# Four layers in one core: rotary rows earlier, layer 0's second context through 128-byte runs, a folded router, and another split of the rotary product

## The chip, the cores and the metric

The kernel runs as one program on one core of a Trainium2 chip. The metric is the device time of one execution in microseconds, as the median of several runs. The core has five engines that run their own instruction streams in order: TensorE (PE, with its weight loads as PEld), VectorE (DVE), ScalarE (ACT), GpSimd (POOL) and SyncE (SP, which here only issues DMAs). An instruction that waits for a semaphore holds everything behind it on its own engine.

## The reference

Eight sequences of 128 tokens with 512 features go through four layers. Each is a cross attention to a context of 128 tokens and a feed-forward block, both added to x; each takes a plain layernorm of x. All is float32.

```python
x = x + L0_xattn(_layernorm(x), ctx, mask0, position_bias, ln_weight, ...)  # 32 heads of 128
x = x + L0_ffn(...)   # 512x512 plus low-rank experts, sparsemax gate
x = x + L1_xattn(...) # 8 small heads over 128-column patches
x = x + L1_ffn(...)   # int8
x = x + L2_xattn(_layernorm(x), ctx, ctx, pos, mask2, Wq, Wk, Wv, Wo)   # 32 q heads, 8 kv heads, rotary
x = x + L2_ffn(...)   # NF4 quantized weights, 1376 hidden
x = x + L3_xattn(...) # 32 q heads, 8 kv heads
x = x + L3_ffn(...)   # router of rank 16 over 64 experts, top 16
```

The parts that the change touches:

```python
# layer 0: the layernorm's result is normed again, and scaled per feature
x = x * rsqrt(mean(x**2) + EPS) * ln_weight        # then q = x @ w_q.T
k = ctx @ w_k.T; v = ctx @ w_v.T
# layer 2: rotary positions
cos, sin = cos_t[position_ids], sin_t[position_ids]
q = q * cos + rotate_half(q) * sin                 # rotate_half: concat(-x2, x1)
k = k * cos + rotate_half(k) * sin
# layer 3, feed-forward: router
q = einsum('bsd,rd->bsr', x, Wq_w)                 # 16 values a token
scores = einsum('bsr,er->bse', q, keys)            # 64 experts
```

## The kernel before

The eight sequences are worked in two halves of four (`HALF`), whose 512 token columns are one moving operand. Attention of layers 0 and 2 runs as a list of 128 units: layer 0's first half (eight groups of four heads), layer 0's second half, layer 2's first half, layer 2's second half. The unit loop is a software pipeline: while unit u is weighed (softmax times values), the scores of u+2 and the projections of u+3 are made. After a group's last head come its four output projections. A tile framework then orders the instructions of each engine and puts in the semaphores; what the source places early or late in the loop is a wish, which the built order follows in the main.

Work that is not attention of the running stage is put in a table by slot (`put(i, f)`); the unit loop calls `slot()` after each piece of projection and after each output projection, two a unit and eight more at a group's end, and each call takes the table's next entry. `drain()` empties the table at the end of a stage. In this way `l0_half(1)` prepares layer 0's second half, from unit 3 on, and `short_stages(hf)` runs layer 0's feed-forward, layer 1's attention and feed-forward and the next norm for half hf under the attention units of the next stage: half 0 under layer 0's second half, half 1 under layer 2's first half. The same calls also hand out steps of the NF4 quantization of layer 2's feed-forward weights, in which ScalarE (`ind`) and VectorE (`dq`) take turns. Those steps last into layer 2's second half. Then come layer 2's feed-forward and layer 3, whose loop runs over items (half, group, sequence) and has its feed-forward put between items by hand (`between`).

A matrix is turned in one of two ways. `transposed` (L191) uses four 128x128 products with the identity on TensorE and a copy out of PSUM. The other way is VectorE's 32x32 block transpose with a DMA that carries blocks: `blocks_sent` and `norm_sent` write blocks to DRAM and read them back in place; `runs_back` and `runs_turned` read 32-element runs of 128 bytes and turn them on VectorE afterwards. `xb_tile` is the layout that the block way leaves, and `chunk` lets a product read either layout.

What the steps of the prediction touch:

- `l0_ctx`, `l0_query`, `l0_turn`: the second half's context is loaded whole and turned on TensorE with a copy by ScalarE; x is loaded, normed twice, turned on TensorE and scaled by `lnw` on VectorE.
- `L1.__init__`: layer 1's weights, 14 small loads on SP, once for each half.
- `L2Inputs`: the mask of layer 2, the positions and the row numbers of all eight sequences; `gather` fetches a sequence's cos and sin rows by an indirect DMA of POOL, `turn` turns them on TensorE. All eight run at the end of `short_stages(0)`.
- `rope` (L711 to L717): VectorE takes the projection from PSUM times cos, then two half products with sin, each from the other half of the partitions; POOL adds. It is called 16 times for keys (L726) and 64 times for queries (L294). The scores (L322) wait for it.
- `F3.route` (L1117 on): four products of `wr` with x give 16 values a token, ScalarE copies them (`qr`), one product with `ke` gives 64 scores, and VectorE picks the top 16. Eight calls, four of them in the last 60 us.
- The SP queue issues nearly all loads of weights (`w`, a ring of 12 buffers; `wo`, 8) in one order with the block transfers.
- PSUM: two banks `mm` for projections in the main stream, three shared by the side work.

Of the kernel before, what the change touches and what calls it, by code (L numbers as in the profile page):

```python
# [62 lines left out]
def kernel(ctx: ExitStack, tc: tile.TileContext, a, out):  # L63
# [187 lines left out]
    def norm_sent(st, b, quarters=False):  # L251
        h = layernorm(st, b)
        view = "p (a b k) -> p a b k" if quarters else "p (b a k) -> p a b k"
# [112 lines left out]
    def l0_ctx(st, b):  # L366
        S.copy(ctxT[:, :, toks(b)], transposed(st, load_ctx(st, b)))
# [11 lines left out]
    def l0_query(st, b):  # L379
        load(x[b], a["x"][b])  # L380
        h = layernorm(st, b)
        r, _ = l0_rms(st, h)
        G.tensor_add(x[b], x[b], h)
        return r

# [131 lines left out]


# [6 lines left out]
    class L1:  # L525
        def __init__(self, st, hf):
# [4 lines left out]
            self.wqk = l1c.tile([P, 3, 64], F32, name="wqk")  # L531
            load(self.wqk, a["l1_wqkv"])
            self.wo = l1c.tile([P, P], F32, name="wo1")
            G.memset(self.wo, 0.0)
            for h in range(8):
                r = 32 * (h % 4) + 8 * (h // 4)
                load(self.wo[r:r + 8, :], a["l1_wo"][8 * h:8 * h + 8, :])
            self.bqk = l1c.tile([P, 1], F32, name="bqk")
            load(self.bqk[0:64, :], a["L1_xattn_bq"].unsqueeze(1))
            load(self.bqk[64:128, :], a["L1_xattn_bk"].unsqueeze(1))  # L540
            self.bv = l1c.tile([P, 64], F32, name="bv")
            load(self.bv, a["L1_xattn_bv"].unsqueeze(0).to_broadcast([P, 64]))
            self.bo = l1c.tile([P, 1], F32, name="bo")
            load(self.bo, a["L1_xattn_bo"].unsqueeze(1))
            hm = l1c.tile([P, 8], F32, name="hm")
            load(hm[64:128, :], a["headmask"])
            self.h4 = l1c.tile([P, 4], F32, name="h4")
            V.tensor_add(self.h4[64:128, :], hm[64:128, 0:4], hm[64:128, 4:8])
# [123 lines left out]
    class L2Inputs:  # L672
        def __init__(self, st):
            self.st = st
            self.pool = tc.tile_pool(name="l2c", bufs=1)
            l2c = self.l2c = self.pool.__enter__()
            mi = l2c.tile([P, B, P], I32, name="mi")
            load(mi, a["mask_ik0"])
            V.tensor_scalar(neg2, mi, 0.0, -BIG, ALU.is_equal, ALU.mult)
            pi = l2c.tile([P, B], I32, name="pi")  # L680
            for b in range(B):
                load(pi[:, b:b + 1], a["pos"][b // HALF, toks(b % HALF)].unsqueeze(1))

            pf = l2c.tile([P, B], F32, name="pf")
            wr = l2c.tile([P, B], F32, name="wr")
# [9 lines left out]
            self.row = l2c.tile([P, B], I32, name="row")  # L695
            V.tensor_copy(self.row, pf)
            self.cs = {}

        def gather(self, b):
# [3 lines left out]
                bass.IndirectOffsetOnAxis(ap=self.row[:, b:b + 1], axis=0))  # L703
# [7 lines left out]
    def rope(dst, mm, t):  # L711
# [3 lines left out]
        V.tensor_mul(r[0:64, :], mm[64:128, :], t[64:128, 1, :])  # L715
        V.tensor_mul(r[64:128, :], mm[0:64, :], t[0:64, 1, :])  # L716
        G.tensor_add(dst, dst, r)  # L717
# [376 lines left out]
    class F3:  # L1094
        def __init__(self, st, hf, f3, wr, ke, wa, wb):
            self.st, self.hf, self.f3, self.wr, self.ke, self.wa, self.wb = st, hf, f3, wr, ke, wa, wb
            self.xT = xt_tile()
            self.h, self.s, self.z, self.zt = {}, {}, {}, {}
# [17 lines left out]
        def route(self, b):  # L1116
            st, f3 = self.st, self.f3  # L1117
            mm = st.mm()
            for c in range(DC):
                T.matmul(mm[:16, :P], lhsT=self.wr[:, c, :], rhs=self.xT[:, c, cols(b)], start=c == 0, stop=c == DC - 1)  # L1120
            qr = f3.tile([16, P], F32, tag="qr", name="qr")
            S.copy(qr, mm[:16, :P])
            sc = st.sc()
            T.matmul(sc[:, 0, :64], lhsT=qr, rhs=self.ke, start=True, stop=True)
# [470 lines left out]
```

## Time and profile before

| what | value |
|---|---|
| median of 3 runs | 3034.03 us (3032.01 to 3035.2) |
| the profiled execution | 3032.72 us |
| its span, first to last instruction | 3030.9 us |
| mean granted TensorE clock | 1.000 |
| DMA read and written | 317.70 MB and 125.33 MB |
| layer 0, first half alone | up to about 550 us |
| layer 2's attention | about 1060 to 1840 us |
| layer 2's feed-forward | about 1840 to 2069 us |
| layer 3 | about 2069 us to the end |

In the profile's groups a line gives the source line, engine, operation and tiles, the count, then busy time and mean duration, then the idle time of the engine just ahead of these instructions and what ended it. A 128x512 float32 product counts as two MATMUL records, whose durations overlap; the distance of their starts is what they take of TensorE's time. In a timeline the columns are start and length in us, engine, line, operation, and in brackets the idle time ahead of it.

### The profile page before, as it was taken

How to read it: one execution, taken by the hardware profiler on the slowest of the kernel's cores; microseconds unless marked ns; L12 is line 12 of the kernel's file. 1: busy time of each engine (PE TensorE's matmuls, PEld its weight loads, DVE VectorE, ACT ScalarE, POOL GpSimd, SP SyncE). 2: the span in 40 equal slices, each digit the busy share in tenths (PEclk: the TensorE clock that was granted, in tenths of full speed). 3: DMA queues.
4: the chain of work that ended last, by engine and by line, in shares of the span. 5: the costliest groups of instructions: out<-in, count | busy, mean ns of one | idle time of the engine just before them, and what ended most of it. 6: DMA issues, size and time to landing. Idle time of an engine off the chain costs nothing.

```text
span 3030.9 us, 35307 instructions
## 1 busy us (share of the span) xinstructions
PE 2999.1 (99%) x10580; PEld 1641.3 (54%) x10584; DVE 1905.8 (63%) x3846; ACT 1336.5 (44%) x3775; POOL 444.7 (15%) x581
## 2 busy tenths in 40 slices
PE   9999999999999999999999999999999999999999
PEld 4544555544444465555555554446566666655554
DVE  5766677667786566887888882215545556555554
ACT  4555565435562433554555561003434343333332
POOL 2000000101110121332111110103111112111111
PEclk9999999999999999999999999999999999999999
DMA  7434444336555633655344433325565656665541
GB/s 219 135 116 123 125 131 122 106 116 169 166 164 164 193 105 98 181 177 169 123 150 122 131 121 105 93 84 157 174 190 174 189 167 196 202 182 175 169 146 47
DMA packets 459006, 445.45 MB, mean 147 GB/s; under 512 B 49568, under 2 KB 347296, under 8 KB 458304
## 3 DMA queue, kind: packets, MB, share of 16 engines
q1 hardware_dynamic: 420896, 357.18, 39.2%
q0 software_dynamic: 14880, 44.06, 5.0%
q10 hardware_dynamic: 23040, 41.95, 4.7%
q8 instruction: 86, 1.41, 0.2%
q14 instruction: 104, 0.85, 0.1%
HBM read 317.70 MB, written 125.33 MB: 146 GB/s over the span
## 4 chain that ended last, share of the span: by engine, by line
PE 86%; DVE 8%; ACT 2%; DMA 2%; issue 1%; POOL 0%; SPq 0%; ACTq 0%; DVEq 0%; POOLq 0%
PE mm L294 18%; PE mm L212 11%; PE tp L1000 7%; PE mm L429 7%; PE mm L1023 7%; PE po L212 7%; PE mm L958 5%; PE sc L1060 4%; PE pv L1083 4%; PE pv L342 3%; PE sc L322 3%; PE mm L967 2%; PE mm L726 1%; DVE dq L803 1%; ACT s L207 1%
## 5 line engine op out<-in xcount | busy, mean ns | idle before, releaser
L212 PE MATMUL mm<-w,o 128*128 128x512 f32 x1024 | 462.6, 595 | 2.1 <-ACT o L344 1.6
L792 ACT ACTIVATE ind<-nw,bounds 128x512 f32<-128x512 f32 (+2 forms) x495 | 345.2, 712 | 239.1 <-DVE dq L803 162.9
L294 PE MATMUL mm<-xT,w 128*128 128x512 f32 x768 | 346.8, 594 | 3.5 <-DVE rot L716 2.3
L803 DVE SCALAR_TENSOR_TENSOR dq<-ind,dq 128x512 f32<-128x512 f32 (+2 forms) x462 | 327.5, 709 | 27.1 <-ACT ind L792 9.1
L212 PEld LDWEIGHTS mm<-w,o 128*128 128x128 f32 x1024 | 188.7, 190 | 221.3 <-issue 206.9
L207 ACT ACTIVATE s<-s,nm 128x128 f32<-128x128 f32 x512 | 198.2, 388 | 100.3 <-DVE nm L313 96.2
L1023 PE MATMUL mm<-w,xT 128*128 128x512 f32 x512 | 234.7, 592 | 0.0
L294 PEld LDWEIGHTS mm<-xT,w 128*128 128x128 f32 x768 | 142.5, 190 | 170.2 <-issue 161.8
L294 PE MATMUL mm<-ctxT,w 128*128 128x512 f32 x512 | 230.3, 593 | 0.8 <-ACT ctxT L1338 0.8
L429 PE MATMUL mm<-w,ctxT 128*128 128x512 f32 x512 | 230.5, 593 | 0.0
L212 PE MATMUL po<-w,o 128*128 128x512 f32 x512 | 229.8, 592 | 0.0
L207 ACT ACTIVATE p<-sc,nm,rq 128x256 f32<-128x256 f32 x256 | 141.0, 560 | 162.2 <-DVE nm L1065 154.9
L160 POOL TENSOR_TENSOR rs<-rs,mhalf 128x1 f32<-128x1 f32 x64 | 38.1, 602 | 871.6 <-DVE rs L181 852.7
L212 PEld LDWEIGHTS po<-w,o 128*128 128x128 f32 x512 | 97.3, 190 | 121.2 <-issue 117.2
L322 PEld LDWEIGHTS sc<-k,q 128*128 128x128 f32 x1024 | 131.5, 191 | 53.9 <-issue 45.1
L1086 ACT COPY o<-pv 128x512 f32<-128x512 f32 x62 | 36.3, 585 | 278.5 <-PE pv L1083 259.2
L1064 DVE TENSOR_REDUCE nm<-sc 128x2 f32<-128x512 f32 x128 | 87.4, 688 | 109.3 <-PE sc L1060 106.8
L429 PEld LDWEIGHTS mm<-w,ctxT 128*128 128x128 f32 x512 | 95.3, 190 | 112.0 <-issue 110.5
L958 PE MATMUL mm<-xB,w 128*128 128x512 f32 (+1 forms) x352 | 152.1, 592 | 0.8 <-DVE x L213 0.8
L213 DVE TENSOR_TENSOR x<-x,mm 128x512 f32<-128x512 f32 x128 | 86.6, 677 | 104.4 <-PE mm L212 104.2
L294 PEld LDWEIGHTS mm<-ctxT,w 128*128 128x128 f32 x512 | 93.5, 190 | 100.4 <-issue 98.6
L344 ACT COPY o<-pv 128x512 f32<-128x512 f32 x128 | 74.2, 579 | 158.0 <-PE pv L342 157.9
(264 smaller groups left out, 4984.8 us busy)
## 6 DMA issues: line engine op xcount, KB each, us to landing
w<-in_l_wq SPq DMA_DIRECT2D x128, 256.0 KB
w<-in_l_wo SPq DMA_DIRECT2D x128, 256.0 KB
far<-tb SPq DMA_DIRECT2D x125, 256.0 KB
pt<-far SPq DMA_DIRECT2D x500, 64.0 KB
far<-tb SPq DMA_DIRECT2D x62, 512.0 KB
pt<-far SPq DMA_DIRECT2D x248, 128.0 KB
far<-tb SPq DMA_DIRECT2D x63, 384.0 KB
pt<-far SPq DMA_DIRECT2D x252, 96.0 KB
```

The lines of the kernel that those rows point to most:

```text
L207: S.activation(dst(h), src(h), AF.Exp, bias=negm[:, h:h + 1], scale=by, accum_out=su[:, h:h + 1])
L212: T.matmul(mm, lhsT=o(h), rhs=wo[h], start=h == 0, stop=h == 3)
L294: T.matmul(mm, lhsT=w[:, c, :], rhs=chunk(xT, c), start=c == 0, stop=c == DC - 1)
L322: T.matmul(sc[:, i, :], lhsT=self.q[:, i * P:(i + 1) * P], rhs=k[:, i * P:(i + 1) * P], start=True, stop=True)
L429: T.matmul(mm, lhsT=ctxT[:, c, toks(self.hf * HALF + i)], rhs=grp.wv[c], start=c == 0, stop=c == DC - 1)
L792: S.activation(ind, w, AF.Relu, bias=bounds[:n, i:i + 1], scale=(down + up)[i][1])
L803: V.scalar_tensor_tensor(dst, ind, step, dst, ALU.min, ALU.subtract if i == len(down) else ALU.add)
L958: T.matmul(mm[:n, :], lhsT=w[c][:, j * P:j * P + n], rhs=chunk(xT, c), start=c == 0, stop=c == DC - 1)
L1000: T.matmul(it.kv[:, s, :], lhsT=lhsT, rhs=it.wkv[c // 2][:, c % 2, :], start=c == 0, stop=c == DC - 1)
L1023: T.matmul(mq, lhsT=self.xT[it.hf][:, c, cols(it.b)], rhs=it.wq[c], start=c == 0, stop=c == DC - 1)
L1060: T.matmul(sc[:, i, :], lhsT=it.qT[2 * j + i], rhs=it.kT, start=True, stop=True)
L1083: T.matmul(pv, lhsT=it.v[:, j, :], rhs=it.pts[j], start=j == 0, stop=j == 1)
```

## The change

Seven edits, in the order of the diff below:

1. Layer 0's second half: the context comes straight from the input in 128-byte runs (`runs_back` on SP, four loads a sequence) and is turned by VectorE; the normed x goes out in blocks and comes back in blocks (`blocks_out`, a piece of `norm_sent` made a function; `norm_arrives`), and `l0_weigh` scales it by `lnw` on POOL. Its tile has the block layout. `l0_half(1)` begins at unit 10 in place of 3, with its steps spread over six slots a sequence in place of four.
2. Layer 1's weights are loaded once, from POOL's queue, at unit 6, into a pool that stays.
3. `L2Inputs` works one half at a time, in three steps: loads, row numbers and gathers, turns. Half 0's loads and gathers begin right after layer 1's attention, its turns at their old place; half 1's stand at the head of `short_stages(1)`.
4. `rope`: ScalarE copies the two halves of the projection, swapped, into `rot`; VectorE multiplies the whole tile by sin; POOL subtracts in place of adding.
5. `F3.route`: `router()`, called once ahead of item 31's other work, makes `wk`, the product of `wr` and `ke` (512 by 64); `route` then has four products with x as the stationary operand and 64 columns of `wk` moving.
6. The three products at the start that warm TensorE read a corner of the block tile.
7. `short_stages` has `turn_rows` and `gather_rows` in the table, and `load_l1` stands beside it.

```diff
@@ -251,4 +251,5 @@
     def norm_sent(st, b, quarters=False):
-        h = layernorm(st, b)
-        view = "p (a b k) -> p a b k" if quarters else "p (b a k) -> p a b k"
+        return blocks_out(st, layernorm(st, b), "p (a b k) -> p a b k" if quarters else "p (b a k) -> p a b k")
+    def blocks_out(st, h, view):
         tb = st.wide("sq" if st.name == "s" else "pt", (P, 4, DC, 32))
@@ -366,3 +367,6 @@
     def l0_ctx(st, b):
-        S.copy(ctxT[:, :, toks(b)], transposed(st, load_ctx(st, b)))
+        return runs_back(st, a["ctx_4096"][b], nc.sync)
+    def l0_ctx_turn(b, t):
+        runs_turned(ctxT[:, :, toks(b)], t)
@@ -385,2 +389,10 @@
+    def l0_send(st, b, r):
+        return blocks_out(st, r, "p (b a k) -> p a b k")
+    def l0_weigh(b):
+        i = 4 * (b % HALF)
+        t = xT0[1][:, i:i + 4]
+        G.tensor_mul(t, t, lnw.unsqueeze(1).unsqueeze(3).to_broadcast([P, 4, DC, 32]))
     def l0_turn(st, b, r):
...
@@ -530,20 +544,3 @@
             l1c = self.pools.enter_context(tc.tile_pool(name="l1c", bufs=1))
-            self.wqk = l1c.tile([P, 3, 64], F32, name="wqk")
-            load(self.wqk, a["l1_wqkv"])
...
-            self.h4 = l1c.tile([P, 4], F32, name="h4")
-            V.tensor_add(self.h4[64:128, :], hm[64:128, 0:4], hm[64:128, 4:8])
+            self.wqk, self.wo, self.bqk, self.bv, self.bo, self.h4 = l1_weights
             self.vt = l1c.tile([P, 4, 8, 32], F32, name="vt")
@@ -672,15 +669,21 @@
     class L2Inputs:
-        def __init__(self, st):
-            self.st = st
+        def __init__(self, st, hf):
+            self.st, self.hf = st, hf
             self.pool = tc.tile_pool(name="l2c", bufs=1)
             l2c = self.l2c = self.pool.__enter__()
-            mi = l2c.tile([P, B, P], I32, name="mi")
-            load(mi, a["mask_ik0"])
-            V.tensor_scalar(neg2, mi, 0.0, -BIG, ALU.is_equal, ALU.mult)
-            pi = l2c.tile([P, B], I32, name="pi")
-            for b in range(B):
-                load(pi[:, b:b + 1], a["pos"][b // HALF, toks(b % HALF)].unsqueeze(1))
+            if hf == 0:
+                self.mi = l2c.tile([P, B, P], I32, name="mi")
+                load(self.mi, a["mask_ik0"])
+            self.pi = l2c.tile([P, HALF], I32, name="pi")
+            for b in range(HALF):
+                load(self.pi[:, b:b + 1], a["pos"][hf, toks(b)].unsqueeze(1))
+            self.cs = {}
+        def rows(self):
+            l2c, pi = self.l2c, self.pi
+            if self.hf == 0:
+                V.tensor_scalar(neg2, self.mi, 0.0, -BIG, ALU.is_equal, ALU.mult)
-            pf = l2c.tile([P, B], F32, name="pf")
-            wr = l2c.tile([P, B], F32, name="wr")
+            pf = l2c.tile([P, HALF], F32, name="pf")
+            wr = l2c.tile([P, HALF], F32, name="wr")
             V.tensor_scalar(wr, pi, 0.0, float(MAXPOS), ALU.is_lt, ALU.mult)
...
@@ -714,5 +716,7 @@
         r = ap_.tile([P, 512], F32, tag="rot", name="rot")
-        V.tensor_mul(r[0:64, :], mm[64:128, :], t[64:128, 1, :])
-        V.tensor_mul(r[64:128, :], mm[0:64, :], t[0:64, 1, :])
-        G.tensor_add(dst, dst, r)
+        S.copy(r[0:64, :], mm[64:128, :])
+        S.copy(r[64:128, :], mm[0:64, :])
+        V.tensor_mul(r, r, t[:, 1, :])
+        G.tensor_tensor(dst, dst, r, ALU.subtract)
...
@@ -1119,9 +1123,5 @@
             for c in range(DC):
-                T.matmul(mm[:16, :P], lhsT=self.wr[:, c, :], rhs=self.xT[:, c, cols(b)], start=c == 0, stop=c == DC - 1)
-            qr = f3.tile([16, P], F32, tag="qr", name="qr")
-            S.copy(qr, mm[:16, :P])
-            sc = st.sc()
-            T.matmul(sc[:, 0, :64], lhsT=qr, rhs=self.ke, start=True, stop=True)
+                T.matmul(mm[:, :64], lhsT=self.xT[:, c, cols(b)], rhs=self.wk[:, c, :], start=c == 0, stop=c == DC - 1)
             s = f3.tile([P, 64], F32, tag="s3", name="s3", bufs=4)
-            V.tensor_copy(s, sc[:, 0, :64])
+            V.tensor_copy(s, mm[:, :64])
             t8 = st.small(8, "t8")
@@ -1253,6 +1253,15 @@
             now[0] = 0
+            def ctx_load(b):
+                box[b, 0] = l0_ctx(side, b)
+            def send(b):
+                box[b, 1] = l0_send(side, b, box[b])
             for i, b in enumerate(batches(hf)):
-                put(4 * i, l0_ctx, side, b)
-                put(4 * i + 1, query, b)
-                put(4 * i + 3, lambda b: l0_turn(side, b, box[b]), b)
+                put(6 * i, ctx_load, b)
+                put(6 * i + 2, query, b)
+                put(6 * i + 4, lambda b: l0_ctx_turn(b, box[b, 0]), b)
+                put(6 * i + 4, send, b)
+                put(6 * i + 7, lambda b: norm_arrives(xT0[1], b, box[b, 1]), b)
+                put(6 * i + 9, l0_weigh, b)
@@ -1268,2 +1277,17 @@
+            def gather_rows(i, hf):
+                put(i, begin, "l2", L2Inputs, hf)
+                call(i + 2, "l2", "rows")
+                for b in batches(hf):
+                    call(i + 3 + b % HALF // 2, "l2", "gather", b)
+            def turn_rows(i):
+                for b in batches(hf):
+                    call(i + b % HALF, "l2", "turn", b)
+                put(i + HALF + 1, lambda: o["l2"].pool.__exit__(None, None, None))
+            if hf:
+                gather_rows(0, hf)
+                turn_rows(10)
             put(0, begin, "f0", F0, hf)
@@ -1292,2 +1316,4 @@
             put(t, lambda: o["l1"].pools.close())
+            if hf == 0:
+                gather_rows(t + 1, hf)
             put(t + 1, begin, "f1", F1, hf)
@@ -1311,7 +1337,25 @@
             if hf == 0:
-                put(t + 1, begin, "l2", L2Inputs)
-                for b in range(B):
-                    call(t + 1 + b, "l2", "gather", b)
-                    call(t + 5 + b, "l2", "turn", b)
-                put(t + 13, lambda: o["l2"].pool.__exit__(None, None, None))
+                turn_rows(t + 1)
+        def load_l1():
+            l1w = sub_pool("l1w", 1)
+            wqk = l1w.tile([P, 3, 64], F32, name="wqk")
+            G.dma_start(wqk, a["l1_wqkv"])
...
+            h4 = l1w.tile([P, 4], F32, name="h4")
+            V.tensor_add(h4[64:128, :], hm[64:128, 0:4], hm[64:128, 4:8])
+            l1_weights.extend((wqk, wo, bqk, bv, bo, h4))
@@ -1328,8 +1372,9 @@
             unit.far = False
-        xT0 += [xt_tile(), xt_tile()]
+        xT0 += [xt_tile(), xb_tile()]
-        V.memset(xT0[1][:, 0, :], 0.0)
+        dummy = xT0[1][:, 0:4].rearrange("p a c j -> p (a c j)")
+        V.memset(dummy, 0.0)
         idle = side.mm()
         for i in range(3):
-            T.matmul(idle, lhsT=xT0[1][:, 0, 0:P], rhs=xT0[1][:, 0, :], start=True, stop=True)
+            T.matmul(idle, lhsT=dummy[:, 0:P], rhs=dummy, start=True, stop=True)
         of = {b: (main, side)[b // 2] for b in batches(0)}
@@ -1364,4 +1409,7 @@
             turning[0] = 8 * NG - 4 <= u < 8 * NG
-            if u == 3:
+            if u == 10:
                 l0_half(1)
+            if u == 6:
+                with tc.issue_after(mark[0].ins):
+                    load_l1()
             if not unit.far:
@@ -1435,2 +1483,16 @@
     load(ke, a["f3_keys"])
+    wk = l3c.tile([P, DC, 64], F32, name="wk3")
+    def router():
+        tp = late.tp()
+        for c in range(DC):
+            T.transpose(tp[:16, c, :], wr[:, c, :], ident)
+        wrt = f3.tile([P, D], F32, tag="z3", name="z3")[:16, :]
+        S.copy(wrt, tp[:16].rearrange("r c p -> r (c p)"))
+        mm = late.mm()
+        for c in range(DC):
+            T.matmul(mm[:, 64 * c:64 * c + 64], lhsT=wrt[:, c * P:(c + 1) * P], rhs=ke, start=True, stop=True)
+        S.copy(wk, mm[:, :4 * 64].rearrange("p (c e) -> p c e", c=DC))
     wa = l3c.tile([P, DC, 512], F32, name="wa")
```

## The prediction

> **What bounds the kernel now.** I read the page's busy row first, then the busy time by stretch, then the waits of TensorE in the one stage that has any, then durations by shape and two timelines.
>
> ```profile
> PE 2999.1 (99%) x10580; PEld 1641.3 (54%) x10584; DVE 1905.8 (63%) x3846; ACT 1336.5 (44%) x3775; POOL 444.7 (15%) x581
> ```
>
> TensorE is without work for 31.8 us of 3030.9. So time goes only if TensorE instructions go, or if one of those 31.8 us goes. Where they lie, by stretch (columns: stretch, length, then busy time of PE, PEld, DVE, ACT, POOL with counts, granted clock, DMA share, GB/s):
>
> ```profile
> 50.00:550.00 500.00, 500.00 (x1578) 255.47 (x1577) 357.34 (x658) 294.53 (x660) 11.30 (x11) 1.00 0.41 121
> ...
> 1220.00:1320.00 100.00, 97.14 (x510) 54.00 (x509) 84.73 (x146) 59.42 (x232) 33.62 (x46) 1.00 0.62 179
> 1320.00:1420.00 100.00, 96.71 (x520) 55.26 (x519) 82.52 (x147) 55.37 (x220) 33.13 (x47) 1.00 0.60 174
> ...
> 1660.00:1760.00 100.00, 99.77 (x398) 57.95 (x397) 84.83 (x134) 59.17 (x168) 16.44 (x12) 1.00 0.44 129
> ...
> 2640.00:2955.00 315.00, 315.00 (x996) 185.68 (x995) 166.74 (x406) 114.74 (x314) 52.57 (x66) 1.00 0.56 171
> ```
>
> In layer 0 (50 to 550) and layer 3 TensorE never stops: there only removed TensorE work counts. In layer 2 (1060 to 1840) the stretches leave 19.6 us idle, with VectorE at 80 to 85% and ScalarE at 55 to 60%. What TensorE waits for there:
>
> ```profile
> PE tp L191 <- DVE h L184: 2.7, 3, 1.3
> PE pv L342 <- DMA pt<-far: 2.5, 3, 1.0
> PE mm L294 <- DVE rot L716: 2.3, 4, 1.2
> PE sc L322 <- POOL q L717: 2.2, 2, 1.2
> PE pv L611 <- DVE s L593: 1.7, 2, 1.1
> ```
>
> No wait is long; most are VectorE coming late, and 4.5 us is the rotary chain itself (rot, then q). The granted clock is 1.00 throughout.
>
> **Layer 0's second context.** Sixteen transposes of the context and sixteen of the normed x leave TensorE.
>
> ```profile
> L191 PE MATMUL tp<-ident,h 128*128 128x128 f32 x84 | 12.6, 275 | 3.2 <-DVE h L184 3.2
> ```
>
> The 275 ns overlap. In the timeline the work behind a group of four starts 0.43 us after the group does (122.08, then 122.51), so 8 groups give 8 x 0.434 = **-3.5 us**, all on the path, since this stretch has no idle. Nothing of it is lost to layout: a 128x512 product that reads the block layout (xB, 596 ns) costs what one with the plain layout does (594). In return VectorE gets eight block transposes (0.70 each) and loses four scalings (0.685): +2.9 us in a stretch where it is 71% busy. ScalarE loses 4 x 0.58. POOL gets 4 products with lnw (1.27 us, like its other 128x512 tensor operations) and, for layer 1's weights, 14 issues of about 0.6 us: some 13 us where it has 11.3 of 500 us busy. SP gets 12 more context issues, 4 of blocks out and 16 back: 32 x 0.43 = 14 us, and loses layer 1's 2 x 14 weight issues. Behind a waiting blocks-out issue SP holds the next w loads; SP's longest wait for a sq tile of VectorE in the first 180 us was 6.0 us. A w tile is one of 12 buffers, its load goes out when TensorE frees one, and eight of the twelve hold key and query weights of 3.44 us of product each, so over 20 us lie between issue and use: I take 0, with bounds 0 and +6. The context lands well ahead of its turn: 64 KB in 128-byte runs (h<-far on POOL's queue) landed in 3.0 us, 7.4 at worst, and the turn comes four slots later; a group takes 62.1 us for 16 slots, so that is 15.5 us.
>
> The Trainium skill, DMA: Bandwidth & Descriptors, Specifications, wants at least 512 B per transfer for line rate; that speaks against 8192 runs of 128 B. The trace has such runs land in 3.0 us, so by the row the sum is as above, and by the rule too unless a load took over 15 us.
>
> **Router folded.** Rows for the router before (L1120, L1124) and for the shape it gets (L578: 64 columns against a 128x128 weight):
>
> ```profile
> L1120 PE MATMUL mm<-xT,wr 128*16 128x128 f32 x64 | 8.4, 274 | 0.0
> ...
> L578 PE MATMUL mm<-wqk,h 128*128 128x64 f32 x64 | 8.1, 270 | 0.0
> ...
> L1124 PE MATMUL sc<-ke,qr 16*128 16x64 f32 x16 | 3.4, 294 | 0.0
> ```
>
> By starts in the timeline, eight L1120 records take 0.98 us and two L1124 0.36, so 1.34 a batch; eight of L578 take 0.84. Eight batches: -4.0. Once, at item 31, the fold costs four transposes (0.43) and eight records like L1124 (0.18 each, 1.4): +1.85. Its second half waits for ScalarE's copy (0.58 plus some 0.2), behind which half of a key projection (0.87) is placed, so the wait is 0; without that cover it is 0.8. In the tail, two waits go or shrink (0.54 for h, 0.51 for z), because ScalarE's copy of qr and the second product leave the chain and a product of 0.86 stands ahead of the transpose: -0.9. Together **-3.0**.
>
> **Rotary rows ahead.** In the one stop of layer 0's end the transpose waits for a row gather just issued:
>
> ```profile
> 996.17 0.41 PE L708 MATMUL tp<-ident,csrow 128*128 128x128 f32 x2 [1.21 <-issue]
> ```
>
> A gather lands 4.4 us after issue. With the gathers five slots (19 us) ahead of the first turn the stop goes: **-1.2**. The second half's four turns move into layer 2's start, the same eight transposes (0.2 each pair) there instead of here: 0.
>
> **Rotary product.** Each of 80 products (16 k, 64 q) had three VectorE steps, then POOL:
>
> ```profile
> L715 DVE TENSOR_TENSOR rot<-mm,cs 64x512 f32<-64x512 f32 x80 | 55.5, 693 | 1.7
> ...
> L713 DVE TENSOR_TENSOR q<-mm,cs 128x512 f32<-128x512 f32 x64 | 43.7, 683 | 47.0 <-PE mm L294 46.9
> ```
>
> Half the partitions cost the same time. Now VectorE has one 128x512 product in place of two halves: -0.69 x 80 = -55 us, 7 points of layer 2's 780 us. ScalarE gets two half copies from PSUM. None is in the trace; the nearest rows are a 128x512 copy from PSUM (L401, 576 ns) and a 64x512 one in SBUF (L567, 617). I take 0.58: 1.16 x 80 = +93 us, 12 points, so ScalarE goes from near 58 to 70% where VectorE goes from 84 to 77%. POOL's subtraction costs what its addition did. The chain of one q head in steady state:
>
> ```profile
> 1626.09 0.69 DVE L713 TENSOR_TENSOR q<-mm,cs 128x512 f32<-128x512 f32 x1 [1.39 <-PE mm L294]
> ...
> 1627.50 0.68 DVE L716 TENSOR_TENSOR rot<-mm,cs 64x512 f32<-64x512 f32 x1
> ...
> 1628.36 1.27 POOL L717 TENSOR_TENSOR q<-q,rot 128x512 f32<-128x512 f32 x1 [10.81 <-DVE rot L716]
> ...
> 1631.11 1.05 PE L322 MATMUL sc<-k,q 128*128 128x128 f32 x8
> ```
>
> From 1626.09 to q's end at 1629.63 it takes 3.54 us, and the scores start 1.48 later. With a free ScalarE the new chain is 1.16 + 0.69 + 1.27 + three hand-overs of about 0.1, 3.4 us: no change. Two heads in each group have this small margin (1.5 and 0.6 us), the other two 8 and 14. Behind the rotary copies on ScalarE stand the copy of o and the exponentials; ahead of them may stand four exponentials (1.7 us), a NF4 step (0.72) or, with layer 1, eight exponentials (4.6 us). What this is worth to TensorE is bounded by -19.6 (every wait goes) and by the second rival's +22. VectorE's lateness is in most waits shown and the relief is 7 points of 84; I take **-3**.
>
> A VectorE product with two SBUF inputs, which the new one is, can be held by POOL:
>
> ```profile
> L420 DVE TENSOR_TENSOR s<-s,su x64: 680/691/1791, 49.6 to 1080.9; 128x512 f32<-128x512 f32 x64
> ```
>
> The 1791 ns one fell on a POOL tensor operation. The rotary operations keep POOL busy 109 of 780 us, so an estimate is 0.14 x 80 x 1.1 = 12 us of VectorE's 55 given back at most, and less, as each POOL step follows its own product. The Trainium skill, GPSIMD Engine Reference, Specifications, says the two engines contend for SBUF when a VectorE instruction has two SBUF inputs; by this rule, as by the row, the relief is 43 to 55 us and the sum stays.
>
> **Sum.** -3.5 - 3.0 - 1.2 - 3 = -10.7. The profiled execution took 3032.72 (span 3030.9, 1.8 around it), 1.3 under the median of 3034.03. So 3022.0 for such an execution, 3023.3 against the median: I say **3023**. Under 0.2% (6 us) this kernel can't be told from unchanged.
>
> **Rivals.**
> - *Layer 2's waits melt.* If VectorE's backlog makes nearly all of them, 80% of 19.6 goes instead of 3: 3034 - 7.7 - 15.7 = 3011. For it: VectorE at 85%, late in most rows. Against: 2.5 us are DMA, and the rotary chain is no shorter.
> - *ScalarE becomes late (slower).* In layer 2 with layer 1, copies queue behind eight exponentials: 8 x (0.388 + 0.187) = 4.6 us, against a margin of 1.3 to 2.3, so 2.8 us of stop each. With half of the 16 blocks there: 8 x 2.8 = 22, giving 3034 - 7.7 + 22 = 3048. It decides from three such stops on. For it: ScalarE in order, VectorE's softmax steps feed it. Against: heads with 8 to 14 us of margin are as many, and the old chain stood in an equally full queue.
> - *Given back.* The 7.7 us of certain removals are met by late weights (SP's +6) or by new waits of a few us: 3032. For it: SP has 32 more issues with waits. Against: 20 us of cover.
>
> **Chances.** Forecast 0.45 (own range 3015 to 3028), melt 0.2, given back 0.15, ScalarE late 0.2. Range: 3006 (melt with all 19.6 us gone) to 3041 (the slow case at two thirds of its price), with a tenth beyond at each end. Faster by over 0.2%: the melt case and most of the forecast, 0.64; within: 0.16; slower: 0.20.
>
> **What would show it.** Right: eight groups of L191 fewer, 50 to 550 still all busy and layer 0 ending some 3.5 us earlier; no stop near 996; L1124 gone; VectorE's share in layer 2 near 77%, ScalarE's near 70%, and less than 19.6 us of TensorE idle there. Wrong: waits of sc or mm for the rotary copies (ScalarE) in layer 2, or waits of products for w in layer 0.

## The result, and the profile after

The changed kernel takes 3023.53 us (median of 8 runs, 3020.5 to 3025.67) where the kernel before took 3033.96 on the same chip (8 runs, 3032.01 to 3035.2). The ratio is 0.9967, 95% interval 0.9958 to 0.9976: 10 us less, against 10.7 in the sum. The profiled execution took 3020.5 us, its span is 3018.7.

To see where the 12.2 us between the two spans lie, take the starts of products that both kernels have: the first output projection (L212) of a group, the first product of layer 2's feed-forward that reads hT (L967 before, L971 after), layer 3's first output projection.

| stretch | before | after | difference | of the sum |
|---|---|---|---|---|
| start to the first group's output projection | 89.42 | 90.64 | +1.22 | 0 |
| from there to the third group's | 127.23 | 124.16 | -3.07 | -3.5 |
| to the fifteenth group's (near layer 0's end) | 812.49 | 812.18 | -0.31 | -1.2 |
| to layer 2's feed-forward | 840.27 | 835.02 | -5.25 | -3 |
| to layer 3's first output projection | 256.69 | 256.69 | 0.00 | 0 |
| to the end | 904.85 | 900.04 | -4.81 | -3.0 |

The total is near, the terms are not. The first row holds 0.3 us by which the kernel after was earlier at its wait near 30 us; from there to the first output projection it is 1.56 us slower. First the busy row of the page after, and the same stretches as before (length, then busy time of PE, PEld, DVE, ACT, POOL):

```profile
PE 2990.5 (99%) x10548; PEld 1638.8 (54%) x10548; DVE 1854.1 (61%) x3778; ACT 1431.9 (47%) x3925; POOL 456.1 (15%) x598
```

```profile
50.00:550.00 500.00, 498.04 (x1549) 252.92 (x1548) 361.53 (x663) 294.60 (x665) 16.57 (x15) 1.00 0.44 130
1220.00:1320.00 100.00, 98.48 (x516) 54.51 (x515) 77.31 (x140) 71.67 (x254) 33.02 (x47) 1.00 0.61 183
1320.00:1420.00 100.00, 94.85 (x501) 53.15 (x500) 74.03 (x135) 66.48 (x237) 32.68 (x46) 1.00 0.56 170
...
1660.00:1760.00 100.00, 99.49 (x402) 57.71 (x401) 77.21 (x121) 74.08 (x194) 15.88 (x12) 1.00 0.43 128
2640.00:2955.00 315.00, 315.00 (x996) 186.97 (x995) 169.23 (x414) 117.96 (x323) 52.30 (x66) 1.00 0.56 170
```

VectorE and ScalarE went where the prediction had them: 74 to 77% and 66 to 74%. TensorE is idle 15.1 us in layer 2 in place of 19.6. But it now stops for 2.0 us in 50 to 550, where it never did. The groups that answer to the ones shown before:

```profile
L720 DVE TENSOR_TENSOR rot<-rot,cs 128x512 f32<-128x512 f32 x80 | 55.1, 689 | 20.5 <-ACT rot L718 20.0
L717 ACT COPY rot<-mm 64x512 f32<-64x512 f32 x80 | 46.7, 583 | 138.6 <-DVE q L715 106.4 <-DVE k L715 28.6 <-DVE lg L485 1.4
L718 ACT COPY rot<-mm 64x512 f32<-64x512 f32 x80 | 46.3, 578 | 1.0
...
L191 PE MATMUL tp<-ident,h 128*128 128x128 f32 x68 | 10.1, 273 | 1.1 <-DVE h L184 1.1
...
L1124 PE MATMUL mm<-wk,xT 128*128 128x64 f32 x64 | 8.0, 268 | 0.0
```

The durations are the predicted ones (0.58, 0.69, eight router records a batch). What ended ScalarE's idle time before L717 is not: VectorE's cos product, 106.4 + 28.6 of 138.6 us, and not the projection on TensorE. The timeline of one head's chain after:

```profile
1578.46 0.69 DVE L715 TENSOR_TENSOR q<-mm,cs 128x512 f32<-128x512 f32 x1 [1.35 <-PE mm L295]
...
1579.24 0.58 ACT L717 COPY rot<-mm 64x512 f32<-64x512 f32 x1 [1.37 <-DVE q L715]
...
1579.83 0.58 ACT L718 COPY rot<-mm 64x512 f32<-64x512 f32 x1
...
1580.55 0.69 DVE L720 TENSOR_TENSOR rot<-rot,cs 128x512 f32<-128x512 f32 x1
...
1581.38 1.27 POOL L721 TENSOR_TENSOR q<-q,rot 128x512 f32<-128x512 f32 x1 [10.82 <-DVE rot L720]
...
1583.48 1.05 PE L323 MATMUL sc<-k,q 128*128 128x128 f32 x8
```

ScalarE was free for 1.37 us and still began only when VectorE had ended: 4.19 us from the cos product's start to q's end, where the kernel before had 3.54. The margin to the scores fell from 1.48 to 0.83 us. TensorE's waits in layer 2 after (engine, line, what is waited for and by which engine; sum, times, longest):

```profile
PE pv L343 <- DMA pt<-far: 2.4, 3, 1.1
PE sc L323 <- POOL q L721: 2.3, 4, 1.4
PE mm L618 <- DVE s L590: 1.9, 1, 1.9
...
PE tp L191 <- DVE h L184: 1.1, 1, 1.1
...
PE mm L295 <- ACT rot L718: 0.3, 1, 0.3
```

The rotary chain's 4.5 us of waits (rot 2.3, q 2.2) became 2.6, although each chain is longer: the waits for rot nearly went, those for q stayed, and VectorE's h went from 2.7 to 1.1.

### The profile page after: what moved, and what is told of

It reads as the page before. It is cut to its first block, busy times and chain, and to the rows that moved or that the text cites. A ratio compares the mean times of both kernels' runs of the same rounds, so it can differ in the third digit from the quotient of the medians.

```text
span 3018.7 us, 35481 instructions
## 1 busy us (share of the span) xinstructions
PE 2990.5 (99%) x10548; PEld 1638.8 (54%) x10548; DVE 1854.1 (61%) x3778; ACT 1431.9 (47%) x3925; POOL 456.1 (15%) x598
## 4 chain that ended last, share of the span: by engine, by line
PE 87%; DVE 5%; ACT 3%; DMA 2%; issue 1%; POOL 1%; SPq 0%; POOLq 0%; ACTq 0%; DVEq 0%
PE mm L295 18%; PE mm L212 13%; PE tp L1004 7%; PE mm L1027 7%; PE po L212 7%; PE mm L441 7%; PE mm L962 5%; PE sc L1064 4%; PE pv L1087 4%; PE pv L343 3%; PE sc L323 3%; PE mm L971 3%; PE mm L730 2%; PE mm L740 2%; ACT s L207 1%
## 5 line engine op out<-in xcount | busy, mean ns | idle before, releaser
L212 PE MATMUL mm<-w,o 128*128 128x512 f32 x1024 | 462.8, 595 | 2.1 <-DVE x L213 1.2
L212 PEld LDWEIGHTS mm<-w,o 128*128 128x128 f32 x1024 | 188.7, 190 | 221.8 <-issue 206.0
L295 PE MATMUL mm<-xB,w 128*128 128x512 f32 x512 | 232.2, 595 | 0.0
L295 PE MATMUL mm<-xT,w 128*128 128x512 f32 x512 | 230.5, 593 | 1.4 <-issue 1.2
L295 PE MATMUL mm<-ctxT,w 128*128 128x512 f32 x512 | 230.2, 593 | 0.8 <-ACT ctxT L1383 0.8
L212 PE MATMUL po<-w,o 128*128 128x512 f32 x512 | 229.8, 592 | 0.0
L1090 ACT COPY o<-pv 128x512 f32<-128x512 f32 x62 | 36.4, 587 | 283.5 <-PE pv L1087 263.4
L212 PEld LDWEIGHTS po<-w,o 128*128 128x128 f32 x512 | 97.3, 190 | 121.2 <-issue 118.1
L295 PEld LDWEIGHTS mm<-xT,w 128*128 128x128 f32 x512 | 95.2, 190 | 111.5 <-issue 109.0
L295 PEld LDWEIGHTS mm<-xB,w 128*128 128x128 f32 x512 | 94.3, 190 | 107.8 <-issue 103.4
```

The lines of the kernel that those rows point to most:

```text
L212: T.matmul(mm, lhsT=o(h), rhs=wo[h], start=h == 0, stop=h == 3)
L295: T.matmul(mm, lhsT=w[:, c, :], rhs=chunk(xT, c), start=c == 0, stop=c == DC - 1)
```

## The experiments

All times stand against the kernel before, run on the same chip; 0.001 of the ratio is 3.0 us. The changed kernel is at 0.9967 and, run again, at 0.9965.

**The old rotary product back.** In `rope` of the changed kernel:

```diff
-        S.copy(r[0:64, :], mm[64:128, :])
-        S.copy(r[64:128, :], mm[0:64, :])
-        V.tensor_mul(r, r, t[:, 1, :])
-        G.tensor_tensor(dst, dst, r, ALU.subtract)
+        V.tensor_mul(r[0:64, :], mm[64:128, :], t[64:128, 1, :])
+        V.tensor_mul(r[64:128, :], mm[0:64, :], t[0:64, 1, :])
+        G.tensor_add(dst, dst, r)
```

> The changed kernel with the old rotary product (three VectorE steps, POOL adds), all else as changed. Theory as predicted (relief of VectorE): TensorE's idle time in layer 2 goes from 15.1 us back to 18 to 20, VectorE's share there from 76 back to about 84%, the time up by 3 to 5 us. Rival (layer 2's 5.2 us came from the weights loaded once and from the rows in two halves, the rotary split is worth nothing): idle 14.5 to 16, time within 1.5 us.

Measured: 3032.14 us, ratio 1.0003 (0.9994 to 1.0012), 11 us above the changed kernel. By the trace 8.8 us lie in layer 2, 1.7 of these in one stretch of half clock (TensorE's granted clock at 0.50 for 3.41 us; the last section has more on it). TensorE's waits in its second half:

```profile
PE mm L295 <- DVE rot L718: 3.4, 6, 1.4
PE sc L323 <- DVE s L753: 2.0, 1, 2.0
PE sc L323 <- POOL q L719: 1.4, 1, 1.4
```

So the rival falls: the new product is worth far more than 3 us here. But the theory's own number, 3 to 5, is passed too, and all the other edits together, with the old product, give no gain (1.0003), though by the sum the router and layer 0's second context alone give 6.5. Something among them costs as much.

**The new rotary product alone**, in the kernel before (the diff above, the other way round).

> The kernel before with the new rotary product alone (ScalarE's two copies, one VectorE sine product, POOL subtracts). In the changed kernel, putting the old product back cost 7.4 us in layer 2 and 1.7 more in one stretch of half clock. Theory (the rotary product is worth all of layer 2's gain and more; the other edits cost layer 2 some 2 us): 5 to 8 us less than before, TensorE's idle time in layer 2 from 19.6 to 12 to 14 us. Rival 1 (as predicted, a small relief): 2 to 4 us less. Rival 2 (the old product is only bad beside the other edits, for instance NF4 steps that come earlier): within 1.5 us of before.

Measured: 3027.81, ratio 0.9985 (0.9976 to 0.9994): 4.5 us less, between theory and rival 1. From the fifteenth group to layer 2's feed-forward the trace gains 3.4 us, with one stretch of half clock in it; 5.1 without. Alone it is worth some 4.5, beside the other edits 11: rival 2 is right in part, and the loss it points to is among the other edits.

**Rotary rows and layer 1's weights alone**: the changed kernel with the old rotary product, old router and old second context, in place of each the lines that the diff takes out.

> The kernel before with only the rotary rows worked by halves and ahead, and layer 1's weights loaded once; old rotary product, old second context, old router. Theory 1 (these edits carry a cost in layer 2 that only the new rotary product covers, since putting the old one back lost 11 us where adding it alone gained 4.5): layer 2 takes 3 to 5 us longer than in the kernel before, the time 2 to 5 us up. Theory 2 (the prediction's step: the stop of 1.2 us goes, nothing else): 0 to 1.5 us down, layer 2 within 1 us. With theory 2 the cost comes from the second context's new path or is the spread between executions.

Measured: 3038.23, ratio 1.0017 (1.0008 to 1.0026), 5.2 us *slower* than before. Theory 1 holds, with a time just past its range: this is the hidden cost. In the trace layer 0's end gains 0.5 us; layer 2's first half loses 1.8 and its second half 2.6 up to the last group, behind which 2.0 come back. The profiled execution was 3.4 us faster than the median, so part of the 5.2 is not in this trace. In the second half no row is worked; its waits are rot 3.4, s 2.0 and q 1.8 us, the first two exactly those of the kernel with only the rotary product put back.

**The same, with the table of short stages as long as before.**

```diff
                 turn_rows(t + 1)
+                put(t + 13, lambda: None)
```

> As the kernel with the rotary rows and layer 1's weights alone, but with an empty entry where half 0's last rotary step stood in the kernel before, so that the table of short stages empties in the same slot and the NF4 steps are handed out as before (939 of their VectorE and ScalarE steps ahead of layer 2, not 960; VectorE's order in layer 2's second half is then that of the kernel before). Theory (the rows themselves cost nothing; their shorter table hands out 21 NF4 steps sooner and so shifts the rest against the heads of layer 2's second half): the waits there are those of the kernel before (rot 2.3 us, q 1.0, s 1.0 in place of 3.4, 1.8 and 2.0), the time 0.5 to 2 us under the kernel before, 5 to 7 under the kernel with the rows alone. Rival (half 1's rows, worked beside layer 1 in layer 2's first half, cost VectorE's time there): still 2 to 5 us over the kernel before.

Measured: 3036.69, ratio 1.0013 (1.0004 to 1.0022). The waits of layer 2's second half:

```profile
PE mm L295 <- DVE rot L718: 2.2, 4, 1.2
PE sc L323 <- POOL q L719: 1.0, 1, 1.0
PE sc L323 <- DVE s L753: 1.0, 1, 1.0
```

In the kernel before they are:

```profile
PE mm L294 <- DVE rot L716: 2.3, 4, 1.2
PE sc L322 <- POOL q L717: 1.0, 1, 1.0
PE sc L322 <- DVE s L751: 1.0, 1, 1.0
```

The waits are those of the kernel before again, and up to the last group that half takes as long as there, to 0.03 us. So the theory is right for this half: the NF4 steps, handed out by slots, had been moved against the heads, which cost 2.6 us there. For the time as a whole it fails: 3.9 us over the kernel before remain, as the rival says, and the median is only 1.3 us under that of the kernel without the padding, with intervals that overlap. In this trace layer 2's first half loses 4.0 us (one stretch of half clock, 1.7, among them) and layer 0's end 0.8. One wait there stands out in both kernels with the rows and weights alone, that of a product for block-turned probabilities from DRAM: the longest is 2.0 and 2.1 us where the kernel before has 1.0. But the new rotary product alone, which moves no rows and no weights, has one of 2.0 us at such a product too. What makes it late stays open: half 1's rows on VectorE and the moved weight loads were not tried apart.

**ScalarE's copies first.** `V.tensor_mul(dst, mm, t[:, 0, :])` is put behind the two copies.

> The changed kernel with ScalarE's two rotary copies issued ahead of VectorE's cos product. Theory (engines that read one projection tile are put one behind the other, whichever comes first): the cos product now starts when the second copy ends, the head chain from projection end to q end stays at 4.2 to 4.6 us, VectorE stands 1.2 us ahead of most of 80 cos products, and the time goes up by 2 to 10 us. Rival (the copies run beside the cos product if they come first, as the prediction's 3.4 us chain had it): chain 3.4 to 3.7 us, the waits for q shrink from 2.3 us, time down by 1 to 3.

Measured: 3026.02, ratio 0.9981 (0.9972 to 0.9990), some 4 us above the changed kernel; the profiled execution has two stretches of half clock (3.4 us), the changed kernel's first profile none. The chain at the head with 0.8 us of margin is 4.25 us long, from the projection's end to q's, where the changed kernel has 4.23. What ended VectorE's idle time before the cos product, and one such chain:

```profile
L718 DVE TENSOR_TENSOR q<-mm,cs 128x512 f32<-128x512 f32 x64 | 43.4, 679 | 10.9 <-ACT rot L717 10.6
```

```profile
1752.59 0.58 ACT L716 COPY rot<-mm 64x512 f32<-64x512 f32 x1 [3.16 <-PE mm L295]
...
1753.19 0.58 ACT L717 COPY rot<-mm 64x512 f32<-64x512 f32 x1
...
1754.04 0.68 DVE L718 TENSOR_TENSOR q<-mm,cs 128x512 f32<-128x512 f32 x1
```

Now VectorE waits for ScalarE; in the chain shown it worked on a score tile just ahead of its product. The two readers of one projection tile stand one behind the other in either order: none of the 80 cos products overlaps a copy, here or in the changed kernel, and the shortest distance is 0.03 us. So the chain holds both, and the rival falls. The theory's 1.2 us of VectorE's time at most products did not come: it waited 10.9 us at the 64 products of q, as other work was put ahead of the rest. That this order is the worse one because VectorE has more behind it is likely, but not shown.

**ScalarE's copies twice.** The two `S.copy` lines of `rope` are repeated, so that each half is written a second time with the same values.

> The changed kernel with ScalarE's two rotary copies made twice (each half written a second time with the same values): 160 more of 0.58 us, ScalarE's share in layer 2's second half from 73 to about 83%, and each rotary chain 1.16 us longer. Theory (chain length matters only at the heads of small slack, now 0.8 and 0.05 us; two of four heads a group late by 0.4 and 1.1 us): 16 groups of up to 1.5, so 10 to 24 us more. Rival (VectorE's load is what sets layer 2's waits, the chain's length does not): at most 5 us more.

Measured: 3057.19, ratio 1.0080 (1.0066 to 1.0094), 34.5 us above the changed kernel on that chip. The waits in layer 2, first half and second half:

```profile
PE sc L323 <- POOL q L723: 6.6, 8, 2.3
...
PE mm L660 <- ACT q8t L655: 2.3, 1, 2.3
```

```profile
PE sc L323 <- POOL q L723: 11.5, 16, 1.9
PE mm L295 <- ACT rot L720: 5.0, 7, 1.2
```

The rival (length does not matter) falls. Chains of 5.4 us leave no margin at two heads of four, and the price passes the theory's 24 us: the projection's tile is also given back late (L295 waits for rot), and 8.5 us of the profiled execution, which was 3.1 us above the median, are half clock. ScalarE's share of the second half rose as well, from 66 to 80%, so the run does not part the chain's length from a busier ScalarE. The changed kernel has little left: its chains of 4.2 us fit, 5.4 do not, and nothing between was run.

**The old router.** `router()` and the folded product go, the four `wr` products, the copy of `qr` and the product with `ke` come back.

> The changed kernel with the old router (four 16-row products, ScalarE's copy, a second product for each of eight batches), all else as changed. By the prediction's step: 8 x 0.5 less TensorE work, 1.85 for the fold, 0.9 in the tail: time up by 3.0. By the difference of the two traces in layer 3: up by 4.8, because besides 0.5 of work a route in the loop also has a gap of some 0.5 us ahead of its second product. Rival (the 1.1 us stop at 2534 of the kernel before was a chance of that execution and the gap is hidden otherwise): up by 1.5 to 2.5.

Measured: 3025.43, ratio 0.9982 (0.9973 to 0.9991), by the ratio 4.5 us more; in the trace layer 3 takes 3.97 us longer. The fold's place (2449 to 2533 us) is 1.42 shorter, and the routes and the tail are 5.39 longer; three of the four routes in the loop cost 0.84 each. One of them with the old router:

```profile
2676.60 3.60 PE L212 MATMUL po<-w,o 128*128 128x512 f32 x8
2680.12 1.05 PE L1124 MATMUL mm<-xT,wr 128*16 128x128 f32 x8
2681.10 0.70 PE L1004 MATMUL tp<-w,ctxT 128*128 128x256 f32 x2
2681.73 0.43 PE L1128 MATMUL sc<-ke,qr 16*128 16x64 f32 x2
2682.09 1.56 PE L1004 MATMUL tp<-w,ctxT 128*128 128x256 f32 x6
2683.49 1.88 PE L1087 MATMUL pv<-pt,v 128*128 128x512 f32 x4
```

Products alone make 0.50 of the 0.84 (starts: 0.98 + 0.36 against 0.84 for the eight new ones). The other 0.34 lies at the seams: the eight products `tp` of w and ctxT next to the route take 2.03 us where the second product cuts them into two and six, 1.78 in the changed kernel where nothing does, and the output projection ahead of the route takes 3.52 in place of 3.43. TensorE is shown busy all along. From the kernel before to the changed one layer 3 gained 0.8 us more than this; there the kernel before waited 1.1 us for a DMA, at 2534 us.

**The old second context**: transposes on TensorE, from unit 3 on.

> The changed kernel with layer 0's second context prepared as before (transposes on TensorE, from unit 3 on). By the prediction's step: 8 groups of 0.434 us back, so 3.5 us more. By the difference of the traces: 3.1 more in the first output group, and the new stop near 52 us (2.0 us) goes, so 1.1 to 1.9 net. Rival (the old path also brings more VectorE products and ScalarE copies): the same, since TensorE never stops there.

Measured: 3025.75, ratio 0.9976 (0.9967 to 0.9986), against 0.9965 for the changed kernel on that chip: 3 us more. In the trace 3.07 us come back between the first and third group, and 0.94 us are saved ahead of them, where the stop near 52 us is gone. The first 30 us differ from one execution to the next; counted from the wait near 30 us, which all 14 profiles have, the first output projection starts 58.96 to 58.97 us later with the old preparation (5 profiles) and 60.5 to 61.5 with the new one (6 profiles, each with a stop of 1.96 to 2.06 us near 52). So up to the third group the old preparation costs only 0.5 to 1.5 us, and the rest of the 3 us does not lie in layer 0 of these traces.

**The changed kernel again**, beside the other runs of that chip.

> The changed kernel once more, as the reference for the other runs of this batch. Expected 0.9958 to 0.9976 of the kernel before. Single times between 3018 and 3026 us would be explained by stretches of half clock after stops in layer 2 with layer 1: each lasts 3.41 us and costs 1.7; a profile without one should be at the low end.

Measured: 3022.72 (3022.1 to 3022.91), ratio 0.9965 (0.9951 to 0.9978). Its profile has one stretch of half clock, starting at 1182 us; the first profile of this kernel, 2.2 us faster, has none.

**The second context's VectorE steps held behind the softmax.** What causes the stop near 52 us? In the timeline of the changed kernel, the softmax's steps (L428, L429, L432) and what stands between them:

```profile
47.90 0.70 DVE L256 STREAM_TRANSPOSE sq<-sq 128x512 f32<-128x512 f32 x1
...
49.09 0.54 DVE L184 TENSOR_SCALAR h<-x,mv,rs 128x512 f32<-128x512 f32 x1
...
51.52 0.49 DVE L380 TENSOR_SCALAR sq<-h,ss 128x512 f32<-128x512 f32 x1 [0.95 <-POOL ss L160]
...
53.85 0.69 DVE L432 TENSOR_TENSOR s<-s,su 128x512 f32<-128x512 f32 x1
...
54.69 0.63 PE L219 MATMUL tp<-ident,s 128*128 128x128 f32 x4 [1.96 <-DVE s L432]
```

L256, L184 and L380 prepare layer 0's second half, which no product needs for hundreds of us: written at unit 10, they run beside the first unit's softmax, because nothing holds them. The edit, in `slot()` (the NF4 steps have the same guard already):

```diff
-            for f, args in table.pop(now[0], []):
-                f(*args)
+            steps = table.pop(now[0], [])
+            if stage[0] == 0:
+                with tc.issue_after(mark[0].ins):
+                    for f, args in steps:
+                        f(*args)
+            else:
+                for f, args in steps:
+                    f(*args)
```

> The changed kernel with the VectorE steps of layer 0's second context put behind the softmax sum of the unit they were written next to, so that they can no longer run 45 to 60 us after the start. Theory (the new stop of 2.0 us near 52 us is softmax standing behind those steps): the stop goes, the first output group starts 1.2 us earlier as in the kernel before, time down by 1 to 2 us, no new stop up to 550. Rival (VectorE lacks the time in any case): as much is lost at another place up to 550, time within 1 us.

> The kernel with the second context's VectorE steps behind the softmax, once more on another chip: 0.9943 to 0.9970 of the kernel before, with no stop near 52 us and the first output group some 1.2 us earlier than in the changed kernel. If the 3.8 us below the changed kernel's profile that the first run showed are real, 3017 to 3020 us on a chip where the changed kernel takes 3022 to 3024.

Measured: 3017.66 (ratio 0.9957, 0.9943 to 0.9970) and 3018.6 (0.9955, 0.9941 to 0.9969), TensorE without a stop from 40 to 560 us and the first output projection 1.60 and 1.71 us earlier; counted from the wait near 30 us it starts after 58.5 us (in both, and with all side work held, below), 2.0 to 3.0 less than in the six profiles with the steps not held. So the theory holds, though the time fell by 3 us where it had 1 to 2. It is the best kernel here, 13 us under the kernel before and 3 under the changed one. Of the 3.8 and 2.3 us by which the two spans are shorter than that of the changed kernel's first profile, 2.2 and 0.6 lie in layer 2 and differ between them. The intervals overlap with the changed kernel's.

**All side work held.** The same guard without the condition on the stage.

> As the kernel with the second context's VectorE steps behind the softmax, but with the VectorE steps of all side work (layer 0's feed-forward, layer 1, norms) held there too. Theory (softmax first also removes layer 2's waits for VectorE's s): TensorE's idle time in layer 2 falls from 13 to 10 us, 1 to 3 us less than with layer 0's steps alone held. Rival (side work then comes late itself, as products that wait for its results, hw, h or km): idle time up by 2 to 10 us.

Measured: 3029.3, ratio 0.9985 (0.9976 to 0.9994), some 9 us above the kernel that holds layer 0's steps alone. The theory falls: side work that is due soon comes late in its turn (rx 1.6 us and hw 1.6 in layer 2, new or longer waits; layer 0's second half alone takes 4.9 us longer than in the changed kernel, 1.7 of it half clock).

## Why the prediction came out right, and where its steps failed

The time, 3023, is the forecast's, but of its four terms only the router's is near what it set. One has the wrong sign, one was mostly given back, and one is far too small and makes up for both. By the runs they are about -1 (second context), -4 (router) and +5 (rows, with layer 1's weights), which add to nothing, as the kernel with the old rotary product measured, and -11 for the rotary product beside them. That the sum was right is luck.

*Layer 0's second context, -3.5.* Right in the size of the gain: seven of the eight groups of transposes lie between the first and the third output projection and gave 3.07, 0.44 each; the eighth lies ahead, and its 0.43 appears once the steps are held (58.5 in place of 58.96 us). No product waited for a weight, so the 0 for SP's 32 more issues held. What failed is "all on the path, since this stretch has no idle" together with VectorE's 2.9 us more "in a stretch where it is 71% busy": I costed the number of VectorE's steps and not their place. The first of them moved from about 80 us to 47, into the first softmax, and took 2.0 to 3.0 us back (60.5 to 61.5 in place of 58.5 us), so that 0.5 to 1.5 of the 3.5 were left.

*Router, -3.0.* Right in mechanism, mis-sized: about -4. The fold measured 1.42 where 1.85 was set. A route saves 0.84 in the loop where 0.50 was set, because 0.34 of it is the change from one kind of product to another, which starts within a group do not show. The tail's -0.9 failed as it was argued: the wait of 0.5 us for h went, but the one for z grew from 0.5 to 1.0 and a new one of 0.4 came; the tail still saved 2.4 us with its four routes.

*Rotary rows ahead, -1.2.* The step that failed. The stop at the gather did go, but TensorE's waits at layer 0's end (940 to 1060 us) after are:

```profile
PE mm L212 <- DVE x L213: 0.9, 1, 0.9
PE mm L660 <- DVE pf L696: 0.5, 1, 0.5
```

So 1.4 us came where 1.2 went. The second wait is put down to the row-number arithmetic (pf), but L660 does not read that: it reads ScalarE's copy q8t, which ended 0.06 us ahead of it, and with the rows and weights alone the wait stands under q8t (0.7 us). With layer 1's weights and nothing else, the edit made the kernel 5.2 us slower. By the traces 2.6 are the shifted NF4 steps in layer 2's second half, which the table's length paces and which the prediction never looked at; the rest is mostly in layer 2's first half, cause open.

*Rotary product, -3.* Too small: 4.5 alone and 11 beside the rows. The chain of "3.4 us: no change" is wrong, since the copies do not run beside the cos product; add that product's 0.69 and the step gives 4.1, measured 4.19. The Trainium skill, PSUM — Partial Sum Buffer, PSUM bank collisions raise a hardware error, says that the compiler's scheduler adds a dependency between any two instructions on different engines that touch one bank and quadrant of PSUM, two reads included; the trace agrees, with ScalarE 1.37 us idle until the cos product ended. At the tightest heads nothing is left of the margin (0.05 us between q's end and the scores, where 0.4 to 0.7 was), and the waits for q are 2.3 us where they were 2.2; the heads that had 1.5 keep 0.8. What is left to explain the gain is VectorE's relief, 51.7 us net by the busy rows, since the chain grew and the time still fell. No run relieves VectorE in another way, so this cause is argued, and why the relief is worth 4.5 us alone and 11 beside the rows stays open. Nothing of it was given back to POOL: the new product took 689 ns on the mean, like the old halves.

*The rivals.* The slow one, ScalarE late, did not come: ScalarE is the releaser of rot for 0.5 us in all of layer 2. The doubled copies show that it was near: 1.16 us more on each chain, and on ScalarE, cost 34.5. "Melt" did not come either, 15.1 of 19.6 us stayed. "Given back" came true for the one edit that seemed safest.

## What to carry to other kernels

An edit that moves work off the critical engine has to be placed in the order of the engine that takes it over: a few early VectorE steps ahead of a softmax cost 2 to 3 of the 3.5 us that the removed transposes gave, and one guard on the order brought that back. Where background steps are handed out by slots of another table, changing that table's length re-times them for hundreds of us; padding it back is a cheap test. Single terms are best measured one edit at a time: here a right total hid a wrong sign. And a chain across engines should be summed with the readers of one PSUM tile one behind the other, whatever engines they are on.

## What the runs showed that was not expected

TensorE's granted clock falls to 0.50 for 3.41 us after some short stops, and this makes part of the spread between executions. In the kernel with rows and padding, first TensorE around such a stop, then the stretches with it (the clock is the number behind the POOL column):

```profile
1313.71 3.60 PE L212 MATMUL mm<-w,o 128*128 128x512 f32 x8
1319.45 1.33 PE L343 MATMUL pv<-pt,v 128*128 128x128 f32 x8 [2.14 <-DMA pt<-far]
1320.58 3.42 PE L212 MATMUL mm<-w,o 128*128 128x512 f32 x4
```

```profile
1310.00:1317.00 7.00, 6.21 (x36) 3.09 (x34) 5.62 (x13) 5.12 (x12) 3.47 (x5) 1.00 0.75 227
...
1320.00:1324.00 4.00, 4.00 (x11) 2.10 (x10) 0.69 (x1) 1.32 (x5) 0.00 (x0) 0.57 0.22 66
```

Four records take 3.42 us behind the stop where eight take 3.60 ahead of it, so each stretch costs 1.7 us beyond the stop (one of 6.83 us twice that). Of 14 profiles 6 have none, 5 have one, the others two, two and four; all but one lie between 1180 and 1470 us, in layer 2 beside layer 1. Not every stop does it: the changed kernel's profile has 1.96 us near 52 without one. In each profile with such stretches their starts, and that of the slow stretch behind the last product, lie multiples of 3.413 us apart, to 3 ns. So it matters how a stop falls on that grid: in the 3.41 us ahead of the stretch shown TensorE worked 1.27, in the grid's window over the stop near 52 us 1.45. Work of 32-row products counts for less, it seems: with the old rotary product 2.4 us of work in the window did not prevent the stretch. The Trainium skill, TensorE: Matmul & The Clock Gate, The HAM clock gate (the "warmup" mystery), has a free-running window of 3413 ns and half rate after at least one idle window; the length and the grid agree, but here a stop of 2.14 us was enough, and in one execution stops of 0.59 and 0.43 us with 32-row products between them.
